# Turned squares of the attention probabilities: sixteen transfers from SBUF to SBUF in the place of five through DRAM

## The chip, the cores and the metric

The kernel runs on one core of one Trainium2 chip. The metric is the device time of one execution in microseconds; the median of three runs stands for it. The engines are called as the profile calls them: PE (matrix multiply; PEld is its weight load), DVE (vector), ACT (scalar), POOL (GpSimd) and SP (sync, which here only issues transfers). A `q` behind a name (SPq, ACTq) marks the engine's own queue of instructions, where transfers are issued and semaphores are waited for.

## The reference

```python
xn = _layernorm(x)                                   # x: 4 x 512 x 512
q = einsum('bpd,hde->bphe', xn, W_Q) + b_Q           # 16 heads of 128; k and v alike
scores = einsum('bqhe,bkhe->bhqk', q, k) / sqrt(128)
attn = softmax(where(causal, scores, -100000.0))
z = einsum('bkhe,bhqk->bqhe', v, attn)
s = einsum('bqhe,hed->bqd', z, W_O) + b_O
g = silu(down(silu(gate(xn) * gate_s) * (up(xn) * up_s)) * down_s)   # 512 -> 1408 -> 512
return x + s * g
```

All of it is float32.

## The kernel before

Every float32 factor of a product is kept as a high and a low part (`Split`, line 28), and a product is three matrix products: high x low, high x high, low x high (`mm3`, line 90). The attention runs first, over 8 groups of 2 heads and, in each group, over the 4 batch rows: 64 rounds, which this text calls heads, of about 14.8 us. The feed-forward part follows from about 973 us on and isn't touched.

The order of the instructions on each engine is the order in which the program writes them (`tc.manual_schedule()`, line 461). One round of the loop at line 525 does, for head n:

- `softmax` (line 272): the scores on PE, the row minimum of the negated scores on DVE (line 298), the exponentials on ACT (line 312), the division by the row sum on POOL (line 316). The causal half is left out, so 10 blocks of 128 x 128 (`NS`) stand in the tile `p`.
- `turn_p` (line 319; line 556 calls it): z needs the probabilities with keys on the partitions. DVE transposes squares of 32 x 32 into the tile `sq` (line 330, six instructions). A square is then turned in itself but still lies on the 32 partitions (`b`) of its queries; it must move to the partitions (`a`) of its keys. That move is what the change is about.
- `split_p` (line 346): reads the moved squares, the tile `ptr`, and makes the high part (ACT, line 357) and the low part (DVE, line 358) in two halves, each of two of the four `b`. From the fifth head on it runs right behind the *next* head's `turn_p`, and in the first heads ahead of it, before or after the softmax.
- the loads of the partial sums of the output (`a`, line 401), of weights (line 130) and of weights to look at (line 438), all issued by ACT; the projections of q and k of the next head on PE, brought out by ACT (line 252) and DVE (line 255); then `attend` (line 376) of the head before, twelve matrix products with `pth` and `ptl`; in every second head `project_out` (line 404) of the four tiles of a batch row, whose sums SP stores (line 414), two in the first half of the round and two in the second.

What bounds the buffers: `sq` has one buffer, so DVE's next transposes (line 330) wait until the moves have read it. `ptr` has two. SP issues its transfers in program order: per head the move of the squares and, in every head after the first few, two stores of line 414.

Semaphores are placed by the framework. In the compiled program every transfer that SP or ACT issues raises one of eight completion counters. They are handed out in rotation over both queues together, in the order in which the compiler lays the instructions out, and a transfer is not issued before the one that last had its counter has landed. An instruction that needs more than its own wait is preceded by instructions that only wait, for up to two counters each.

Of the kernel before, what the change touches and what calls it, by code (L numbers as in the profile page):

```python
# [10 lines left out]
F32 = mybir.dt.float32  # L11
# [31 lines left out]
def kernel(  # L43
# [21 lines left out]
    nc = tc.nc  # L65
# [10 lines left out]
    dram = ctx.enter_context(tc.tile_pool(name="dram", bufs=1, space=bass.MemoryType.DRAM))  # L76
# [19 lines left out]
    with ExitStack() as at:  # L96
# [169 lines left out]
        Q = 32  # L266
        NQ = P // Q
        NS = NT * (NT + 1) // 2
# [50 lines left out]
        def turn_p(of):  # L319

            sq = pp.tile([P, NQ, NS, Q], F32, name="sq", tag="sq")
            for pack in PACK:
                for t in pack:
                    for j in range(0, t + 1, 2):
                        n = min(2, t + 1 - j)
                        s0 = slot[j] + t - j
                        step = slot[j + 1] + t - j - 1 - s0 if n > 1 else 1
                        src = of[t][:, j * P : (j + n) * P]
                        dst = sq[:, :, s0 : s0 + (n - 1) * step + 1 : step, :]
                        nc.vector.transpose(  # L330
                            dst.rearrange("p a s i -> p s a i"),
                            src.rearrange("p (s a i) -> p s a i", s=n, i=Q),
                        )
            by_query = dram.tile([NQ, Q, NQ, NS * Q], F32, name="turn", tag="turn", bufs=2)
            nc.sync.dma_start(
                out=by_query.rearrange("b j a s -> (b j) (a s)"),
                in_=sq.rearrange("p a s i -> p (a s i)"),
            )
            raw = pp.tile([P, NQ, NS * Q], F32, name="ptr", tag="ptr", bufs=2)
            for a in range(NQ):  # L340
                nc.sync.dma_start(
                    out=raw[ts(a, Q)], in_=by_query[:, :, a, :].rearrange("b j s -> j b s")
                )
            return raw

        def split_p(raw):
# [114 lines left out]
        with tc.manual_schedule():  # L461
# [57 lines left out]
            inexact, before, raw = None, None, None  # L519
# [5 lines left out]
            for n, (g, b, i) in enumerate(heads):  # L525
# [27 lines left out]
                half = NT // 2 if nxt is not None else NT - 1  # L553
                fill(range(0, half))
                if nxt is not None:
                    raw_next = turn_p(of)
# [38 lines left out]
                if nxt is not None:  # L595
                    *_, kT = project(nxt[1], nh, wk[nh], bk_sb, "k")
                    raw = raw_next
# [206 lines left out]
```

## Time and profile before

| what | us |
|---|---|
| median of the three runs | 1223.08 (1222.31 to 1223.1) |
| the profiled execution's own time | 1222.41 |
| its span in the profile | 1220.6 |
| issues of line 335, 640 KB each | 63, median 3.8 to landing |
| issues of line 341, 160 KB each | 252, median 3.4 to landing |
| DMA traffic over the span | 215.55 MB, mean 177 GB/s |

The span runs from the first to the last instruction of the profiled execution; a time is compared with a time, a span with a span. A busy figure is the time in which an engine had an instruction at work. Counts behind an x are instructions. A line of the stretches view gives, after the stretch and its length, the busy times of PE, PEld, DVE, ACT and POOL with their counts, PE's granted clock, the share of time in which the 16 DMA engines were busy, and the GB/s that they moved. A line of a timeline gives start, duration, engine, line and operation; instructions of one kind in a row are merged, and "x4" is then four of them. A line of the wait list says who waited for whom: the total, how often, the longest.

### The profile page before, as it was taken

The numbers are of one execution on the slowest core, as the hardware profiler recorded it, in microseconds if no ns is written. First come the engines' busy times: TensorE is split into PE (matmuls) and PEld (weight loads), VectorE is DVE, ScalarE is ACT, GpSimd is POOL, SyncE is SP. The second block draws the span as 40 slices with busy tenths as digits, with TensorE's granted clock in tenths as the row PEclk, the third lists the DMA queues.
The fourth block names the chain that finished last, engine by engine and source line by source line (L and its number), as shares of the span: only waits on it lengthen the run. The fifth ranks groups of instructions, "written<-read, shape, count | busy, mean of one in ns | idle before, by whom it ended". The sixth has DMA issues, their size and how long they took to land.

```text
span 1220.6 us, 18887 instructions
## 1 busy us (share of the span) xinstructions
PE 1206.5 (99%) x6514; PEld 1052.7 (86%) x6514; DVE 827.1 (68%) x2044; ACT 525.3 (43%) x1169; POOL 301.7 (25%) x433
## 2 busy tenths in 40 slices
PE   8999999999999999999999999999999999999997
PEld 8888888888888888888888888888888888888886
DVE  6897777777777777777877676767677533434343
ACT  5654444444445445444544454445444342323231
POOL 4212321232123213321412141214121341212010
PEclk9999999999999999999999999999999999999999
DMA  4454456656665667566655565555544893627241
GB/s 161 138 175 147 145 165 206 206 179 190 190 207 174 203 198 218 181 208 192 211 182 173 178 189 175 177 185 173 173 156 156 272 317 93 207 87 213 80 147 38
DMA packets 117912, 215.55 MB, mean 177 GB/s; under 512 B 13232, under 2 KB 45744, under 8 KB 117808
## 3 DMA queue, kind: packets, MB, share of 16 engines
q1 hardware_dynamic: 74016, 134.51, 34.4%
q10 hardware_dynamic: 29376, 53.26, 14.2%
q0 software_dynamic: 14416, 26.48, 7.9%
q8 instruction: 53, 0.87, 0.3%
q14 instruction: 51, 0.42, 0.1%
HBM read 135.17 MB, written 79.04 MB: 175 GB/s over the span
## 4 chain that ended last, share of the span: by engine, by line
PE 95%; DVE 3%; ACT 1%; DMA 0%; issue 0%; SPq 0%; DVEq 0%; ACTq 0%
PE z L387 10%; PE pd L667 7%; PE pg L667 7%; PE pu L667 7%; PE pso L91 5%; PE psv L91 5%; PE pso L92 5%; PE pso L93 5%; PE psv L93 5%; PE psv L92 5%; PE psq L91 5%; PE psq L92 5%; PE psq L93 5%; PE psk L91 5%; PE psk L92 5%; PE psk L93 5%
## 5 line engine op out<-in xcount | busy, mean ns | idle before, releaser
L316 POOL TENSOR_SCALAR p<-p,rtot 128x512 f32<-128x512 f32 (+3 forms) x256 | 148.2, 598 | 675.1 <-DVE rtot L315 675.1
L312 ACT ACTIVATE p<-p,nmax 128x512 f32<-128x512 f32 (+3 forms) x256 | 140.9, 552 | 147.3 <-DVE nmax L298 147.3
L358 DVE TENSOR_TENSOR ptl<-ptr,pth 128x640 fp32r<-128x640 f32 x126 | 133.7, 1099 | 1.4 <-ACT pth L357 1.4
L330 DVE STREAM_TRANSPOSE sq<-p 128x256 f32<-128x256 f32 x378 | 113.3, 361 | 0.0
L298 DVE CUSTOM_DVE_ANT_0 p<-sc,mask 128x512 f32<-128x512 f32 (+2 forms) x192 | 96.5, 552 | 0.3 <-PE sc L93 0.3
L252 ACT ACTIVATE k<-psk,consts 128x512 fp32r<-128x512 f32 (+1 forms) x65 | 44.2, 681 | 108.7 <-PE psk L93 108.6
L252 ACT ACTIVATE q<-psq,consts 128x512 fp32r<-128x512 f32 (+1 forms) x65 | 44.3, 682 | 97.2 <-PE psq L93 72.6
L357 ACT CAST pth<-ptr 128x640 fp32r<-128x640 f32 x126 | 84.9, 724 | 0.1
L413 DVE TENSOR_TENSOR a<-pso,a 128x512 f32<-128x512 f32 x108 | 72.1, 686 | 17.7 <-PE pso L93 16.4
L255 DVE SCALAR_TENSOR_TENSOR k<-psk,consts,k 128x512 fp32r<-128x512 f32 (+1 forms) x65 | 48.0, 739 | 52.8 <-ACT k L252 52.7
L693 DVE SCALAR_TENSOR_TENSOR hd<-pu,consts,sg 128x512 f32<-128x512 f32 x44 | 33.0, 751 | 66.8 <-PE pu L667 62.2
L315 DVE RECIPROCAL rtot<-tot 128x1 f32<-128x1 f32 x256 | 41.6, 162 | 42.7 <-ACT p L312 36.3
L91 PE MATMUL sc<-k,q 128*128 128x512 f32 (+2 forms) x192 | 65.7, 342 | 1.7 <-DVE xl L225 1.7
L93 PE MATMUL sc<-k,q 128*128 128x512 f32 (+2 forms) x192 | 64.7, 337 | 0.0
L92 PE MATMUL sc<-k,q 128*128 128x512 f32 (+2 forms) x192 | 64.7, 337 | 0.0
L255 DVE SCALAR_TENSOR_TENSOR q<-psq,consts,q 128x512 fp32r<-128x512 f32 (+1 forms) x65 | 47.6, 732 | 7.6 <-ACT q L252 7.6
L312 ACT ACTIVATION_READ_ACCUMULATOR p<-p,nmax 128x1 f32 x256 | 47.8, 187 | 0.0
L91 PEld LDWEIGHTS sc<-k,q 128*128 128x128 f32 x192 | 36.2, 188 | 7.9 <-DVE xl L225 3.5
L723 ACT ACTIVATE o<-o 128x512 f32<-128x512 f32 (+1 forms) x17 | 10.3, 607 | 68.8 <-DVE o L722 68.8
L92 PEld LDWEIGHTS sc<-k,q 128*128 128x128 f32 x192 | 36.2, 189 | 3.6
L93 PEld LDWEIGHTS sc<-k,q 128*128 128x128 f32 x192 | 36.1, 188 | 2.6
L691 ACT ACTIVATE sg<-pg,consts 128x512 f32<-128x512 f32 x44 | 30.3, 688 | 17.0 <-PE pg L667 17.0
(734 smaller groups left out, 3811.6 us busy)
## 6 DMA issues: line engine op xcount, KB each, us to landing
turn<-sq SPq DMA_DIRECT2D x63, 640.0 KB, 3.8
ptr<-turn SPq DMA_DIRECT2D x252, 160.0 KB, 3.4
acc<-a SPq DMA_DIRECT2D x124, 256.0 KB, 3.7
a<-acc ACTq DMA_DIRECT2D x108, 256.0 KB, 2.8
xt<-in_x SPq DMA_DIRECT2D x16, 256.0 KB, 4.1
wor<-in_w_o ACTq DMA_DIRECT2D x16, 256.0 KB, 4.5
fa<-acc SPq DMA_DIRECT2D x16, 256.0 KB, 5.9
fx<-in_x SPq DMA_DIRECT2D x16, 256.0 KB, 6.9
```

Source lines behind the costliest of these rows:

```text
L91: nc.tensor.matmul(ps, a.hi, b.lo, start=first, stop=False)
L92: nc.tensor.matmul(ps, a.hi, b.hi, start=False, stop=False)
L93: nc.tensor.matmul(ps, a.lo, b.hi, start=False, stop=last)
L252: nc.scalar.activation(q.hi[:, at_], ps[:, at_], AF.Identity, bias=bias[:, h : h + 1])
L255: nc.vector.scalar_tensor_tensor(q.lo[:, at_], ps[:, at_], bias[:, h : h + 1], q.hi32[:, at_], ALU.add, ALU.subtract,)
L298: nc.vector.tensor_tensor_reduce(out=of[t], in0=where[t], in1=add, scale=-SCALE, scalar=BIG, op0=ALU.add, op1=ALU.min, accum_out=nmax[t],)
L312: nc.scalar.activation(of[t], of[t], AF.Exp, bias=nmax[t], scale=-1.0, accum_out=tot)
L316: nc.gpsimd.tensor_scalar(of[t], of[t], rtot, 1.0, ALU.mult, ALU.mult)
L330: nc.vector.transpose(dst.rearrange("p a s i -> p s a i"), src.rearrange("p (s a i) -> p s a i", s=n, i=Q),)
L358: nc.vector.tensor_tensor(dst(pt.lo), src, dst(pt.hi32), ALU.subtract)
L387: nc.tensor.matmul(o, v, p_, start=k == 0, stop=k == len(todo) - 1)
L667: nc.tensor.matmul(ps, l, r, start=first and k == 0, stop=last and k == len(pairs) - 1)
```

## The change

The sixteen blocks (four key parts `a` by four query parts `b`) are copied one by one from `sq` to `ptr`, 32 partitions with a row of 320 elements (1280 bytes) each. The DRAM tile `turn` is gone. All sixteen are issued by SP, those of the first two `b` ahead of the others.

```diff
@@ turn_p, line 334
-            by_query = dram.tile([NQ, Q, NQ, NS * Q], F32, name="turn", tag="turn", bufs=2)
-            nc.sync.dma_start(
-                out=by_query.rearrange("b j a s -> (b j) (a s)"),
-                in_=sq.rearrange("p a s i -> p (a s i)"),
-            )
             raw = pp.tile([P, NQ, NS * Q], F32, name="ptr", tag="ptr", bufs=2)
-            for a in range(NQ):
-                nc.sync.dma_start(
-                    out=raw[ts(a, Q)], in_=by_query[:, :, a, :].rearrange("b j s -> j b s")
-                )
+            for half in range(2):
+                for a in range(NQ):
+                    for b in (2 * half, 2 * half + 1):
+                        nc.sync.dma_start(
+                            out=raw[ts(a, Q), b, :],
+                            in_=sq[ts(b, Q), a].rearrange("p s i -> p (s i)"),
+                        )
             return raw
```

## The prediction

> **What bounds the kernel now.** I read the page's head and its table by slices first, then busy time by stretches, then PE's own waits.
>
> ```profile
> span 1220.6 us, 18887 instructions
> PE 1206.5 (99%) x6514; PEld 1052.7 (86%) x6514; DVE 827.1 (68%) x2044; ACT 525.3 (43%) x1169; POOL 301.7 (25%) x433
> ...
> 35.00:45.00 10.00, 9.27 (x46) 7.43 (x45) 9.18 (x27) 5.17 (x14) 2.05 (x4) 1.00 0.44 157
> ...
> 60.00:100.00 40.00, 38.33 (x221) 32.98 (x220) 35.57 (x100) 22.02 (x49) 5.64 (x9) 1.00 0.50 156
> 100.00:240.00 140.00, 140.00 (x780) 123.44 (x779) 105.79 (x270) 63.51 (x151) 38.50 (x50) 1.00 0.56 178
> 240.00:600.00 360.00, 360.00 (x2029) 318.75 (x2028) 274.83 (x702) 165.53 (x389) 97.09 (x120) 1.00 0.64 197
> 600.00:960.00 360.00, 360.00 (x2019) 317.95 (x2018) 259.73 (x694) 165.84 (x392) 87.40 (x122) 1.00 0.55 175
> ```
>
> From 100 to 960 us PE is busy for all of the 860 us, at a granted clock of 1.00. While the turned squares are in use (27 to 960 us) PE idles only 0.73 us between 35 and 45 and 1.67 us between 60 and 100: 2.4 us together. The wait list gives these to DVE (`PE sc L91 <- DVE xl L225: 1.7, 4, 0.6` is the largest), none to a transfer of the squares. So removing work around the squares can win at most 2.4 us; the question is whether the new transfers make PE wait.
>
> One head in the middle, from the timelines of SP, DVE and ACT (start, duration, engine, line, what):
>
> ```profile
> 488.62 0.32 SPq L335 DMA_DIRECT2D turn<-sq  x1
> 492.06 1.74 SPq L341 DMA_DIRECT2D ptr<-turn  x4
> 494.86 1.71 SPq L414 DMA_DIRECT2D acc<-a  x2
> ...
> 500.45 0.73 ACT L357 CAST pth<-ptr 128x640 fp32r<-128x640 f32 x1
> ...
> 500.93 1.80 DVE L330 STREAM_TRANSPOSE sq<-p 128x256 f32<-128x256 f32 x6
> 502.65 1.52 DVE L358 TENSOR_TENSOR ptl<-ptr,pth 128x640 fp32r<-128x640 f32 x2
> ...
> 502.76 0.32 SPq L335 DMA_DIRECT2D turn<-sq  x1
> ```
>
> Call T the moment the squares leave (488.62). The last piece back was issued by T+5.2, the first cast that reads it runs at T+11.8, and the next head's transposes refill sq at T+12.3. I read the same marks off all 62 gaps between one turn and the next: medians T+5.6, T+11.6 and T+13.0, a period of 14.8 us; the earliest cast is T+8.1 (first head), the earliest refill T+10.4 (fourth). From T+5.6 plus a landing time (next view) to T+11.6 lie some 2.6 us of slack.
>
> **The change, part by part.** Landing times and issue costs, from the views of tiles sq and ptr and of line 341, and two rows of SP's wait list:
>
> ```profile
> L335 SPq DMA_DIRECT2D turn<-sq x63: 319/320/338, 27.1 to 947.0; - x63
> DMA to landing us min/median/max: 2.9/3.8/6.4
> ...
> L341 SPq DMA_DIRECT2D ptr<-turn x252: 302/424/1266, 30.1 to 953.5; - x126
> L341 SPq EVENT_SEMAPHORE  x97: 17/28/4845, 30.0 to 947.4; - x97
> DMA to landing us min/median/max: 2.3/3.4/5.9
> ...
> SPq L341 <- DMA turn<-sq: 230.0, 63, 6.1
> SPq L414 <- DMA ptr<-turn: 0.8, 1, 0.8
> ```
>
> *Removed:* per head one 640 KB write, four 160 KB reads, and SP's wait for the write (230.0 / 63 = 3.65 us). Nothing of it lies on PE's path: value zero, bounds 0 and -2.4 us. The DMA engines lose half of the squares' traffic (640 KB per head each way), which relieves the weight loads; those too are waited for by nobody on PE's list.
>
> *Added:* sixteen issues of 40 KB (32 rows of 1280 B). Four ptr issues take 1.74 us, of which the last is 0.42, so starts are 0.44 apart; sixteen need 7.04 us where five and a wait needed 5.6. Bounds for one issue are 0.30 and 1.27; I take 0.44, the row with the same row length on the same queue. Landing: no row shows SBUF to SBUF. Bounds are 2.3 and 6.4 from the two tiles; I take 2.3, the fastest 160 KB piece, because a piece is now a quarter of that and no longer shares 1.74 us with three others. Last landing T+7.04+2.3 = T+9.3, with 2.3 us to the median cast and 3.7 to the median refill. The first cast needs only the first eight: T+5.8.
>
> The wait rows speak of what else can delay: an acc store (L414) waited for ptr, which it neither reads nor writes. That is the rotation of eight completion counters over the transfers of SP and ACT together. With sixteen transfers the ninth and later ones of a head wait for earlier ones. If two of the eight are held by ACT's loads and the acc stores, six are left: 16/6 x L of latency plus 6 x 0.44 = 2.6 us. With L = 2.3 that is T+8.7, less than the 9.3 of issuing, so the counters don't bind.
>
> *Moved on SP:* the two late acc stores (T+6.2 here) now queue behind the sixteenth issue, T+7.0 plus; in the first two heads four x loads do. The `a` buffer of such a store is wanted again two heads later, over 20 us on; x of those loads is read by statistics 8 us later or more. Cost nothing.
>
> *Moved on ACT:* ACT issues its loads of a, weights and look ahead of T (500.39 to 501.68 for T=502.76; 4.7 to 2.8 us ahead in the other kind of head). By the compiled order of before, these now share the rotation with the first few of the sixteen and with the stores just ahead, so the last of a head's ACT loads waits for a store issued up to 1.4 us before T (landing 3.7, so about T+2.3) or for the first to fourth new transfer (T+2.7 to T+4.1). Behind it in ACT's queue stand the evictions of q and k (502.99 and 505.71), the last of which feeds the scores at 510.24: k needs ACT 0.69 and DVE 0.75, so may start as late as T+6.0, q 0.7 before it. Holding ACT to T+2.3 or T+4.1 is covered by that; beyond T+5 PE pays one for one.
>
> *Other waits:* the casts, the subtracts and the refill each wait for up to eight counters, two to an instruction, where one to two instructions were enough: some ten waits of 21 to 28 ns per head on DVE and ACT, 0.25 us, hidden under PE from 100 us on. In the DVE-bound first 100 us (DVE 35.57 of 40 us busy) at most 4 x 0.25 = 1.0 us shows; I take 0.3. In the first head the second cast (35.9 us) would start at 27.08+9.3 = 36.4, 0.5 late, but its subtract starts at 37.9 behind another: covered by 0.8.
>
> The Trainium skill speaks against the change: its page "DMA: Bandwidth & Descriptors", section "Rules for kernel authors", says that transfers below 64 KB pay mostly overhead and should be merged, and the page's fit of 2.0 us plus bytes over 436 GB/s makes 2.1 us of 40 KB. Paid one after another that would be an estimate of 33.5 us a head, 20.5 beyond the refill, 62 times: 1270 us more. The rows above show four transfers issued within 1.74 us and landing after 3.4, so the overhead overlaps and the rule's serial reading does not hold here.
>
> *Sum:* span 1220.6 + 0.3 = 1220.9. The profiled execution took 1222.41, 1.8 more than its span; the median of the runs shown, 1223.08, is 0.67 above that. Forecast: 1223.08 + 0.3 = 1223.4.
>
> **The rivals.**
> *A, the sixteen land too late.* Place: the refill of sq and the casts of the next head. If a small transfer takes L = 4.0 rather than 2.3, the counters bind: 16/6 x 4.0 + 2.6 = T+13.3, against a median refill at T+13.0: 0.3 x 62 = 19 us, 1242. It decides from L = 3.9; turn's median of 3.8 is close, ptr's 3.4 gives T+11.7 and nothing. With L = 5 it would be T+15.9 and 180 us. An issue of 0.67 instead of 0.44 (16 x 0.67 + 2.3 = 13.0) does the same without the counters. Against it: 3.8 belongs to 640 KB.
> *B, ACT is held.* Place: ACT's loads of look and weights, which stand before the evictions. If the store or transfer ahead on the counter lands 1.5 us later than I think, ACT is held to T+5.6, 0.6 past the point; in the twenty or so heads with looks and weights this is 12 us: 1235. For it: stores have landed in 3.7 at the median, not the minimum. Against it: k's eviction waits 2.03 us for PE anyway.
> *C, faster.* Less traffic brings the first 100 us forward by up to all of PE's 2.4 us: 1220.7. Against it: those waits are for DVE.
>
> **How the numbers follow.** Forecast 0.60, A 0.20, B 0.15, C 0.05. About 0.2% (2.4 us) is what a measurement of this kernel can tell from no change; the forecast lies within, A and B above, C at the lower edge. Faster 0.05, same 0.60, slower 0.35. The range goes from 1221.5 to 1245: it holds the forecast, B's 1235 and A's 1242, and leaves out A's upper half (0.10), B's tail (0.03) and C (0.05).
>
> **What would show it.** Right: PE busy 360.00 in both long stretches, sixteen issues on SP some 7 us long, landings near 2.3, casts still at T+11 to T+12.6, and no PE wait on ptl or pth. Wrong: SP idle on new transfers within the sixteen and landings near 4 (A); q and k evictions later than T+5 with PE waiting on k's low part (B); the waits on xl gone (C). A piece issue far from 0.44 us would break the sum first.

## The result and the profile after

The changed kernel takes 1233.71 us (median of six runs, 1230.01 to 1238.04); the kernel before took 1222.97 beside it (six runs, 1221.77 to 1223.79). The ratio is 1.009, with a 95% interval of 1.0069 to 1.011: slower by 10.7 us. The runs of the changed kernel scatter over 8 us, those of the kernel before over 2. The profiled execution is the slowest of the six (1238.04, span 1236.3), so its losses are at the upper end of what a run shows.

The head of its page:

```profile
span 1236.3 us, 19954 instructions
PE 1212.9 (98%) x6514; PEld 1056.2 (85%) x6514; DVE 830.3 (67%) x2044; ACT 528.7 (43%) x1169; POOL 300.0 (24%) x433
```

The stretches of the changed kernel, with the same columns as before the change (length, busy PE, PEld, DVE, ACT, POOL, granted clock, DMA share, GB/s):

```profile
60.00:100.00 40.00, 36.30 (x201) 31.27 (x200) 33.83 (x94) 20.37 (x42) 7.12 (x10) 0.96 0.37 107
100.00:240.00 140.00, 139.95 (x790) 123.55 (x789) 105.64 (x275) 65.03 (x153) 33.39 (x45) 1.00 0.41 123
240.00:600.00 360.00, 355.69 (x1973) 313.05 (x1973) 270.14 (x685) 162.66 (x380) 96.73 (x120) 1.00 0.49 149
600.00:960.00 360.00, 359.99 (x2028) 318.19 (x2028) 263.07 (x694) 166.95 (x394) 90.38 (x124) 1.00 0.43 133
```

PE was busy for all of 240 to 600 us; now it idles 4.31 us there. DMA traffic fell as expected (149 GB/s where it was 197), and nobody profits. Where a head loses is found by setting the start of the first z product of each of the 64 heads against that of the kernel before. Of the 15.7 us between the spans, 1.2 lie at the start, before any square has moved; 6.3 lie in the second and fourth heads (2.45 and 3.89); 7.7 in seven heads between the fifteenth and the thirty-ninth, of which one alone has 3.41 and one 1.90. What is left, 0.5, is spread in steps under 0.15 and behind the last z product.

The new transfers, and who waits for them (view of the tile ptr, durations in ns; then the wait list):

```profile
L338 SPq DMA_DIRECT2D ptr<-sq x1008: 507/589/1739, 28.3 to 972.5; - x168
...
DMA to landing us min/median/max: 1.8/1.9/6.1
```

```profile
ACT pth L355 <- DMA ptr<-sq: 24.8, 23, 3.0
DVE sq L330 <- DMA ptr<-sq: 13.6, 14, 2.4
PE z L385 <- DVE ptl L356: 4.2, 4, 1.7
PE sc L91 <- DVE k L255: 3.7, 2, 2.1
SPq L338 <- DMA acc<-a: 18.8, 18, 2.5
```

An issue takes 0.589 us where I had taken 0.44, and with the time between two of them starts are 0.63 apart: the sixteen span 10.0 us from the first start to the last end at best, 10.6 at the median of the 63 sets and 13.5 at the longest. A piece lands 1.9 us after its issue, faster than the 2.3 that I had taken. DVE and ACT now wait for the pieces, and PE waits four times for the low part that DVE makes of them. Its two waits for k, 3.7 us together, stand ahead of the z products of the second and the fourth head; before, the scores never waited for k.

The head that loses most after the fourth, from the timelines of SP, ACT, POOL, DVE and PE (start, duration, engine, line, what; in brackets the idle time before it and what ended it):

```profile
289.51 13.48 SPq L338 DMA_DIRECT2D ptr<-sq  x16
...
304.31 0.73 ACT L355 CAST pth<-ptr 128x640 fp32r<-128x640 f32 x1 [2.17 <-DMA ptr<-sq]
...
305.64 3.11 POOL L135 TENSOR_TENSOR wo2l<-wor,wo2h 128x512 fp32r<-128x512 f32 x2 [3.79 <-ACT wo2h L134]
...
304.37 1.81 DVE L330 STREAM_TRANSPOSE sq<-p 128x256 f32<-128x256 f32 x6 [2.42 <-DMA ptr<-sq]
306.10 3.33 DVE L356 TENSOR_TENSOR ptl<-ptr,pth 128x640 fp32r<-128x640 f32 x2
...
309.49 0.50 PE L385 MATMUL z<-ptl,v_0h 128*128 128x512 f32 x1 [1.66 <-DVE ptl L356]
```

T is 289.51. The sixteen end at T+13.5, the refill of sq starts at T+14.9 after 2.42 us of waiting, and the two subtracts behind it on DVE take 3.33 us, because POOL splits weights at the same time; PE stands for 1.66 us. In the kernel before the subtracts of this head were just as slow, but started in time; its timelines of DVE and PE:

```profile
295.50 3.56 DVE L358 TENSOR_TENSOR ptl<-ptr,pth 128x640 fp32r<-128x640 f32 x2
...
299.57 0.40 PE L387 MATMUL z<-ptl,v_0h 128*128 128x512 f32 x1
```

They ended at 299.06 and PE read them at 299.57: in this head the cover is 0.5 us, not the two or more of a head in which the pair takes 1.52. In 21 of the 64 heads POOL splits weights beside the subtracts, and all the losses after the fourth head stand in the z product of such a head or are first seen at the start of the next one.

The stall costs PE more than its own 1.66 us. The stretches of five microseconds around it (the granted clock is the third number from the end):

```profile
305.00:310.00 5.00, 3.34 (x18) 2.68 (x17) 5.00 (x8) 2.34 (x5) 3.11 (x2) 1.00 0.77 230
310.00:315.00 5.00, 5.00 (x29) 4.96 (x29) 1.93 (x4) 1.27 (x3) 0.00 (x0) 0.66 0.24 64
315.00:320.00 5.00, 5.00 (x26) 4.30 (x26) 4.12 (x16) 3.70 (x11) 2.24 (x4) 1.00 0.28 68
```

In the next stretch of 5 us the granted clock is 0.66, which is another 5.00 x 0.34 = 1.7 us. 1.66 + 1.7 = 3.4, this head's whole loss.

### The profile page after: what moved, and what is told of

Its sections match the earlier page's. It is cut to its first block, busy times and chain, and to the rows that moved or that the text cites. A ratio compares the mean times of both kernels' runs of the same rounds, so it can differ in the third digit from the quotient of the medians.

```text
span 1236.3 us, 19954 instructions
## 1 busy us (share of the span) xinstructions
PE 1212.9 (98%) x6514; PEld 1056.2 (85%) x6514; DVE 830.3 (67%) x2044; ACT 528.7 (43%) x1169; POOL 300.0 (24%) x433
## 4 chain that ended last, share of the span: by engine, by line
PE 77%; SPq 9%; DMA 6%; DVE 4%; ACT 2%; issue 1%; ACTq 0%; DVEq 0%
SPq L338 8%; PE z L385 8%; PE pd L665 6%; PE pg L665 6%; PE pu L665 6%; PE psv L91 4%; PE pso L91 4%; PE psv L93 4%; PE psv L92 4%; PE pso L93 4%; PE pso L92 4%; PE psq L91 3%; PE psq L92 3%; PE psq L93 3%; PE psk L91 3%; PE psk L92 3%
## 5 line engine op out<-in xcount | busy, mean ns | idle before, releaser
L330 DVE STREAM_TRANSPOSE sq<-p 128x256 f32<-128x256 f32 x378 | 113.7, 365 | 14.8 <-DMA ptr<-sq 13.6
L355 ACT CAST pth<-ptr 128x640 fp32r<-128x640 f32 x126 | 88.9, 725 | 28.3 <-DMA ptr<-sq 24.8
L411 DVE TENSOR_TENSOR a<-pso,a 128x512 f32<-128x512 f32 x108 | 72.1, 687 | 17.7 <-PE pso L93 17.0
L255 DVE SCALAR_TENSOR_TENSOR k<-psk,consts,k 128x512 fp32r<-128x512 f32 (+1 forms) x65 | 48.0, 739 | 42.2 <-ACT k L252 42.0
L91 PE MATMUL sc<-k,q 128*128 128x512 f32 (+2 forms) x192 | 66.6, 347 | 5.5 <-DVE k L255 3.7
L255 DVE SCALAR_TENSOR_TENSOR q<-psq,consts,q 128x512 fp32r<-128x512 f32 (+1 forms) x65 | 47.8, 736 | 12.6 <-ACT q L252 12.6
L91 PEld LDWEIGHTS sc<-k,q 128*128 128x128 f32 x192 | 36.5, 190 | 12.3 <-DVE k L255 4.9
L721 ACT ACTIVATE o<-o 128x512 f32<-128x512 f32 (+1 forms) x17 | 10.3, 607 | 68.8 <-DVE o L720 68.8
```

The source lines that it names most:

```text
L91: nc.tensor.matmul(ps, a.hi, b.lo, start=first, stop=False)
L255: nc.vector.scalar_tensor_tensor(q.lo[:, at_], ps[:, at_], bias[:, h : h + 1], q.hi32[:, at_], ALU.add, ALU.subtract,)
L330: nc.vector.transpose(dst.rearrange("p a s i -> p s a i"), src.rearrange("p (s a i) -> p s a i", s=n, i=Q),)
```

## The experiments

My theory after the first look: what decides is the moment at which the queue that issues the sixteen is done with them, against the refill of sq and the casts. At 0.63 us a piece that moment comes some 3 us later than I had worked out, and the cover is used up. Rivals: the counters and the transfers that share them; the acc stores and the x loads that were moved back on SP; sixteen transfers from SBUF to SBUF costing by their number, whoever issues them. Twelve kernels tell these apart. In the diffs, lines with "-" are those of the changed kernel.

**What makes an issue dear.** The squares go to DRAM as before, and come back in sixteen pieces of the same 32 rows of 1280 bytes.

```diff
+            nc.sync.dma_start(out=by_query..., in_=sq...)
...
-                            in_=sq[ts(b, Q), a].rearrange("p s i -> p (s i)"),
+                            in_=by_query[b, :, a, :],
```

> The write to DRAM as before, but sixteen reads of 40 KB (32 rows of 1280 bytes) in the place of four of 160 KB: the shape of the new pieces with the source of the old ones. If the 0.59 us that one new issue takes comes from SBUF on both sides, an issue here takes about 0.44 us as before and the sixteen take some 7 us; if it comes from the shape of 32 short rows, 0.59 us and 10 us. The last piece lands at T+3.0+7.0+2 = T+12 in the first case and T+15 in the second, against refill at T+13 (which here needs only the write) and casts at T+11.6: some 10 us slower than before in the first case, over 60 us in the second, as the casts then come 3 us late in every head.

The tile's view:

```profile
L343 SPq DMA_DIRECT2D ptr<-turn x1008: 302/419/1922, 30.3 to 971.0; - x168
...
DMA to landing us min/median/max: 1.7/1.9/4.8
```

Same rows, same bytes, same queue: 0.419 us from DRAM, 0.589 from SBUF; of the two issue times the shorter came. So the pair of memories, not the shape of 32 rows, makes the issue 0.17 us dearer, and 0.44 was near the right price, for the wrong kind (starts are 0.46 apart here). The run took 1237.55 us (one run). The casts are late here, in 60 heads by 2.0 us on average (`ACT pth L357 <- DMA ptr<-turn: 122.3, 60, 4.1`), and yet the z products are only 15.1 us behind at the last head, 6.3 of them in the second to fourth heads. So with sq free early a late cast alone is mostly covered from the fifth head on; the first four lose by it as much as in the changed kernel (6.4).

**Which heads lose.** The new move in the first four heads only, and from the fifth on only.

```diff
-        def turn_p(of):
+        def turn_p(of, head):
+            if head < 4:   # the other kernel: head >= 4
...
+            else:          # through DRAM, as before
```

> The sixteen transfers in the first four heads only, the five through DRAM in all others. If the loss of the changed kernel's first four heads (2.45 + 0.12 + 3.89 = 6.5 us by the starts of z) belongs to these heads and is not made later, about 6.5 us remain: 1228 to 1231. If the loss is one of the long middle alone and the early part is chance, 1223 to 1224.

> The five through DRAM in the first four heads, the sixteen transfers in the other 59. The rest of the loss is then left: 7.8 us in the profiled run, in heads 14 to 38, so 1226 to 1231, and e2 and e3 together make up the whole change. If the early heads push the later ones into their loss, 1223 to 1225.

The first: 1228.21 us (1226.91 to 1230.21), ratio 1.0041 (1.0027 to 1.0055), 5.6 us. The second: 1229.19 (1228.33 to 1231.31), ratio 1.0055 (1.0038 to 1.0072), 6.6 us. Together 12.2, where the whole change costs 10.7. Half of the cost belongs to four heads out of 64, those in the DVE-bound first 100 us. The other half lies in few of the sixty heads, seven in the profiled execution of the second kernel, by 0.3 to 2.2 us, and all seven come right behind weight splits.

**More transfers.** The four pieces that go to the last key part are cut in two: twenty a head.

```diff
-                        nc.sync.dma_start(...)
+                        src = sq[ts(b, Q), a].rearrange("p s i -> p (s i)")
+                        cuts = (0, 160, 320) if a == NQ - 1 else (0, 320)
+                        for lo, hi in zip(cuts, cuts[1:]):
+                            nc.sync.dma_start(out=raw[ts(a, Q), b, lo:hi], in_=src[:, lo:hi])
```

> Twenty transfers: the four pieces of the last a are moved in two halves of 640 bytes a row. If the issue rate decides, SP's chain is 20 x 0.63 = 12.6 us at the least, the last piece lands at T+13.9, the refill takes 1.8 more, and no head can be shorter than 15.7 us, where 14.8 is the mean before: 0.9 x 60 = 54 us and the first heads' loss on top, some 1280 to 1300, more where a transfer waits for its counter. If the loss is one of single unlucky heads, four more transfers add a few us: 1235 to 1240.

1348.93 us (1348.53 to 1349.96), ratio 1.1041 (1.1022 to 1.1059). Four more issues cost 115 us more than the sixteen did, 1.8 per head, more than the size that I had expected. Its wait list:

```profile
DVE sq L330 <- DMA ptr<-sq: 153.1, 50, 5.1
...
PE z L385 <- DVE ptl L356: 59.0, 40, 2.8
```

The refill waits in 50 heads, and PE stands 59.0 us for the low part; the rest of the loss is the lower clock behind the stalls (0.973 over the span) and other waits. Sixteen stood at the edge; twenty are past it in nearly every head.

**Fewer issues on SP, without touching another queue.** The first two `b` move from SBUF to SBUF in eight pieces, the other two through DRAM in one write and four reads.

```diff
-            for half in range(2):
+            half = NQ // 2
...
+            nc.sync.dma_start(out=by_query..., in_=sq[half * Q :]...)
             for a in range(NQ):
-                    for b in (2 * half, 2 * half + 1):
+                for b in range(half):
                     nc.sync.dma_start(out=raw[ts(a, Q), b, :], in_=sq[ts(b, Q), a]...)
+            for a in range(NQ):
+                nc.sync.dma_start(out=raw[ts(a, Q), half:, :], in_=by_query[:, :, a, :]...)
```

> The pieces of the first two b go from SBUF to SBUF in eight transfers, the others through DRAM in one write ahead of them and four reads behind them: 13 issues on SP, 0.3 + 8 x 0.63 + 4 x 0.44 = 7.1 us, sq free at T+7.3, the last piece at T+9.2. If the issue rate of the sixteen is the cause, nothing is late from the fifth head on and the time is 1223 to 1226. If any use of transfers between SBUF and SBUF on this queue hurts, half of the loss stays: about 1228.

1222.08 us (1221.41 to 1223.52), ratio 1.0003 (0.9993 to 1.0012): the time of before. The stretches:

```profile
240.00:600.00 360.00, 360.00 (x2029) 318.72 (x2028) 275.21 (x702) 166.09 (x389) 97.08 (x120) 1.00 0.56 174
600.00:960.00 360.00, 360.00 (x2019) 317.92 (x2018) 260.51 (x694) 166.44 (x392) 87.37 (x122) 1.00 0.50 153
```

**The rotation of the counters.** ACT's loads and the acc stores are issued by POOL, so that the sixteen share their counters with hardly anything.

```diff
-                nc.scalar.dma_start(out=a, in_=acc_d[b][t])
+                nc.gpsimd.dma_start(out=a, in_=acc_d[b][t])
-            nc.sync.dma_start(out=acc_d[b][t], in_=a)
+            nc.gpsimd.dma_start(out=acc_d[b][t], in_=a)
```

(and the weight and look loads alike)

> The sixteen transfers in all heads, but the loads of a, of weights and of looks and the acc stores are issued by POOL, so that in the attention the rotation of the eight counters on SP holds almost nothing but the sixteen. If it is the shared counters that delay the last pieces of heads 14 to 38 by 0.5 to 3.5 us, the sixteen take 10.0 us in every head, land at T+12 and the loss of the middle goes: about 1229 to 1230, of which 6.5 are the first heads. If the cost of sixteen issues is enough by itself, the loss stays at 1233 to 1235.

1259.24 us (1257.07 to 1262.13), ratio 1.0304 (1.0283 to 1.0325): neither case. The sixteen still span 10.0 to 12.8 us, since SP now waits for its own earlier pieces (`SPq L338 <- DMA ptr<-sq: 26.8, 36, 2.2`). The transfers given to POOL made new waits: PE waits 13.7 us for the low part, and 9.3 once at the start of the feed-forward part, whose first loads POOL issued late. A narrower try moves the stores alone:

```diff
-            nc.sync.dma_start(out=acc_d[b][t], in_=a)
+            nc.gpsimd.dma_start(out=acc_d[b][t], in_=a)
```

> Only the stores of the partial sums go from SP to POOL; ACT's loads stay. If the 256 KB stores between the sets of sixteen (their issues and the completion counters that they hold) push the sixteen past the refill in single middle heads, SP needs 10.1 us for the sixteen in nearly all heads, the losses after the fourth head (8 to 10 us) fall to 3 or less, and the time is 1228 to 1231. If the sixteen issues alone or ACT's loads cause them, the losses stay and the time is 1232 to 1236. Both keep the 6 us of the first four heads.

1261.49 us (1258.41 to 1264.17), ratio 1.0319 (1.0301 to 1.0337): again neither case. The spans of the sixteen hardly changed (46 heads under 11 us where there were 38, the longest 12.7 where it was 13.5). Two timeline rows of POOL and one of DVE show what came instead:

```profile
504.29 1.13 POOL L412 DMA_DIRECT2D acc<-a  x2
505.44 2.54 POOL L135 TENSOR_TENSOR wv4l<-wvr,wv4h 128x512 fp32r<-128x512 f32 x2
...
505.94 5.93 DVE L356 TENSOR_TENSOR ptl<-ptr,pth 128x640 fp32r<-128x640 f32 x2
```

The stores put POOL's four weight splits 1.13 us later, right beside the subtracts, which now take 5.93 us for the pair; the head loses 3.98. Five such heads (pairs of 5.6 to 5.9 us) lose 16 us together. These two kernels say that the counters' other users don't set the chain's length; what they say of the losses is clouded by POOL.

**The x loads.** They leave SP for POOL; and, in a second kernel, the splits of the second to fourth heads also come behind their transposes, as they do from the fifth on.

```diff
-            nc.sync.dma_start(out=xt, in_=x[b, ts(t, P), :])
+            (nc.sync if b == 0 else nc.gpsimd).dma_start(out=xt, in_=x[b, ts(t, P), :])
# second kernel also:
-                early = n < HG * HG or nxt is None
-                if n == 1:
-                    pt = split_p(raw)
+                early = n == 0 or nxt is None
```

> Only the x loads of the second to fourth batch row go from SP to POOL, so that they no longer stand behind the sixteen issues. If the late x loads make the early losses (6.3 us over heads 1 and 3 of the changed kernel), these fall to about 3 and the time to 1229 to 1231. If the early losses come from the late casts and refills of the squares themselves, they stay at 6 and the time at 1232 to 1236.

> The sixteen transfers in all heads, but the x of the later batch rows is loaded by POOL, ahead of nothing of SP, and heads 1 to 3 split their squares behind their own transposes, as the later heads do. If the loss of the first heads comes from casts and statistics that stand too near behind the squares' last piece, 5 to 7 us of the loss go: 1226 to 1230, the loss of heads 14 to 38 remaining. If it comes from something else in the first heads, 1232 to 1236.

The first: 1236.0 us (1233.58 to 1238.11), ratio 1.0115 (1.01 to 1.0131). The second: 1233.37 (1229.97 to 1236.6), ratio 1.0088 (1.0061 to 1.0114), a miss. In neither do the statistics wait for x any more between 25 and 100 us, where the changed kernel has `DVE st L187 <- DMA xt<-in_x: 1.3, 2, 0.8`. With x alone the second to fourth heads still lose 5.1 us in the profiled execution, beside 6.4; with the splits moved too, 2.8. So the late x loads are not what the early heads lose by; the place of the splits is a part of it. The second kernel's total didn't follow, because its later heads lost some 10 us, where the changed kernel's profile has 7.7.

**Eight pieces on another queue.** The second half is issued by POOL, so SP's chain is 5 us long.

```diff
-                        nc.sync.dma_start(
+                        (nc.sync, nc.gpsimd)[half].dma_start(
```

> The eight transfers of the first two b stay on SP, the eight of the others are issued by POOL at the same time. If the loss comes from one queue issuing sixteen at 0.63 us each, SP's chain is 5.0 us, the last piece lands near T+7 to T+9, no refill waits, and the time is that of before to within 2 us: 1222 to 1226. If the transfers between SBUF and SBUF themselves are slow, or the sharing of counters with ACT's loads is what counts, it stays above 1230.

1259.02 us (1257.93 to 1259.97), ratio 1.03 (1.0283 to 1.0317), 37 us: a miss. All of the loss lies in seven heads, every eighth (4.0 to 7.6 us each); the other 57 lose nothing but 0.9 at the start. The timelines of POOL and ACT in one of the seven:

```profile
487.85 3.52 POOL L338 DMA_DIRECT2D ptr<-sq  x7 [2.54 <-DVE sq L330]
494.14 0.50 POOL L338 DMA_DIRECT2D ptr<-sq  x1 [2.78 <-PE psv L93]
494.65 1.27 POOL L135 TENSOR_TENSOR wq8l<-wqr,wq8h 128x512 fp32r<-128x512 f32 x1
495.87 1.27 POOL L135 TENSOR_TENSOR wk8l<-wkr,wk8h 128x512 fp32r<-128x512 f32 x1
...
495.96 0.34 ACTq L130 DMA_DIRECT2D wqr<-in_w_q  x1
...
498.04 0.69 ACT L252 ACTIVATE q<-psq,consts 128x512 fp32r<-128x512 f32 x1 [10.78 <-POOL wk8l L135]
```

POOL's transfers stand ahead of its weight splits, the eighth 2.78 us late; ACT's next load into wqr waits until the split has read it; and q's eviction, behind that load in ACT's queue, starts 10.78 us after ACT's last work. What held the eighth transfer isn't settled: the row names a product that it doesn't read.

**Twelve pieces and four copies.** The four blocks with a equal to b keep their partitions, so POOL copies them, ahead of the splits too.

```diff
-                        nc.sync.dma_start(...)
+                        src = sq[ts(b, Q), a].rearrange("p s i -> p (s i)")
+                        if a == b:
+                            nc.gpsimd.tensor_copy(raw[ts(a, Q), b, :], src)
+                        else:
+                            nc.sync.dma_start(out=raw[ts(a, Q), b, :], in_=src)
```

> The four blocks that keep their partitions (a equal to b) are copied by POOL, and only twelve are transferred, with no DRAM between. If the length of SP's chain is what counts, 12 x 0.63 + 1.9 - 0.1 = T+9.4 for the last landing, as early as with half of the move through DRAM, and the time is that of before, 1221.5 to 1224, PE busy 360.0 in both long stretches. If transfers from SBUF to SBUF cost the time by something other than the length of the chain (counters, ACT's loads held up, SBUF traffic), three quarters of them leave 5 us or more: 1228 and above. A rival of its own: POOL's copies, in order among its other work, come later than the transfers, and the refill waits for them: 1226 or more with DVE waiting on POOL.

1231.93 us (1231.64 to 1232.92), ratio 1.0078 (1.0064 to 1.0092): a miss. Nobody waits for a transfer of ptr in the steady part. The loss again lies in seven heads, the same ones as with eight pieces on POOL, 0.9 to 1.7 us each (the third head loses another 1.0), and PE waits for k there (`PE sc L91 <- DVE k L255: 7.1, 7, 1.5`). The copies, 2.95 us for the four, stand where POOL's transfers stood.

**All sixteen, with POOL's eight behind the splits.** This is the run that separates the length of the chain from all the rest.

```diff
-                        nc.sync.dma_start(
-                            out=raw[ts(a, Q), b, :],
-                            in_=sq[ts(b, Q), a].rearrange("p s i -> p (s i)"),
-                        )
+                        src = sq[ts(b, Q), a].rearrange("p s i -> p (s i)")
+                        if half == 0:
+                            nc.sync.dma_start(out=raw[ts(a, Q), b, :], in_=src)
+                        else:
+                            later.append((raw[ts(a, Q), b, :], src))
...
                 split_pending(n)
+                for dst, src in later:
+                    nc.gpsimd.dma_start(out=dst, in_=src)
+                later.clear()
```

> All sixteen pieces, eight issued by SP and eight by POOL, but POOL's eight after the round's weight splits. If only the length of one queue's chain costs, and the 37 us of the kernel with eight on POOL ahead of the splits came from the splits behind them, every head is covered (SP done at T+5, POOL's last issue at some T+8, landing by T+10) and the time is 1221.5 to 1225. If sixteen transfers cost by their number whoever issues them (counters, landings), losses of the changed kernel's size stay: 1230 or more.

1222.02 us (1221.73 to 1223.34), ratio 0.9997 (0.9988 to 1.0006): the time of before. Its timelines of SP, POOL and DVE in one of the heads that lost most with the other order:

```profile
489.78 4.96 SPq L342 DMA_DIRECT2D ptr<-sq  x8
...
490.06 1.88 POOL L135 TENSOR_TENSOR wq9l<-wqr,wq9h 128x512 fp32r<-128x512 f32 x1
491.90 1.87 POOL L135 TENSOR_TENSOR wk9l<-wkr,wk9h 128x512 fp32r<-128x512 f32 x1
493.71 3.98 POOL L562 DMA_DIRECT2D ptr<-sq  x8
...
489.63 2.99 DVE L359 TENSOR_TENSOR ptl<-ptr,pth 128x640 fp32r<-128x640 f32 x2
```

The subtracts are as slow as ever beside the splits (2.99), the pieces are the same sixteen, and they land later than in the changed kernel (2.3 us at the median, where it was 1.9). But SP is done at T+5, POOL at T+7.9. Sixteen transfers cost nothing by their number; one queue issuing them for 10 us and more does.

This kernel settles a rival that the two on the rotation left clouded. POOL's pieces take their counters from a set of eight of POOL's own, so it could be the easier rotation that helped, and not the shorter chain. But SP waited more for the stores here than in the changed kernel (18.8 us in 18 places there):

```profile
SPq L342 <- DMA acc<-a: 31.7, 26, 2.8
```

Single sets of SP's eight take up to 8.4 us where 4.9 is the least. So the waits for counters are still there, and behind a chain of 5 us they cost nothing.

Open: a second buffer for sq, which should take the refill's wait away, wasn't tried. That a loss needs both the late chain and the slow subtracts is read from the traces; no kernel moved the splits away from the subtracts. Why the losing heads differ from run to run isn't known.

## Why the prediction was right or wrong

The forecast of 1223.4 us, held at 0.60, missed by 10.3. The 1233.71 lies inside the range only because the range was drawn wide enough for the rivals, and that it stands near B's 1235 is luck: B's mechanism did not come.

*PE as the bound, nothing to gain: right.* No kernel is faster than before by more than its interval. PE is busy for all of 100 to 960 us before, so a move that is done in time is worth nothing; the relief of the DMA engines shows (149 for 197 GB/s) and buys no time.

*"sixteen need 7.04 us": wrong, and this is the step that failed.* I took 0.44 us for an issue, the row with the same row length on the same queue, which was a read from DRAM. Measured: 0.589, starts 0.63 apart, 15 x 0.63 + 0.59 = 10.0 us where no piece waits. The first kernel shows why that row didn't carry over: the same pieces read from DRAM cost 0.419. My own bounds (0.30 to 1.27) held it; the choice between them was by shape, and the kind of memory decided. The prediction did name this: a piece issue far from 0.44 would break the sum first.

*Landing 2.3: close, on the safe side.* It was 1.9. Without a wait the last of the sixteen starts at T+9.45 and lands at T+11.4, not at T+9.3; the median of the 63 sets lands at T+12.1. Heads whose refill of sq doesn't wait start it mostly at T+12.1 to T+13.5, so some 1 to 2 us of cover are left, where I had counted 3.7 to the median. The Trainium skill's fit, cited in the prediction, gave 2.1 for the landing; its page has it for transfers issued by GpSimd, and these were issued by SP. The rows have 1.9, and the serial reading remains refuted, since sixteen pieces were done within some 11.4 us.

*"so the counters don't bind": wrong in single heads.* SP waits 18.8 us in 18 places for acc stores within the sixteen (2.5 at most), which together with single slow issues (up to 1.74) stretches the ten microseconds to 13.5 in the worst heads. This is a part of the cause in the middle: in six of the seven heads that lose there the sixteen take 11.8 to 13.5 us and land at T+13.1 to T+14.8, past a refill due at some T+12.4, which the T+11.4 of issuing alone would have met. In the first head no piece waits, and the length of the issues is enough by itself. Freeing the rotation of other users hardly shortened the chain, as SP then waited for its own pieces. With the 7.04 us that I believed in, even the longest stretch of 3.5 gives a landing at 7.04 + 3.5 + 1.9 = T+12.4, just in time, which is an estimate.

*Moved on SP: "cost nothing" was right for the time.* The x loads did come later and were waited for, by 1.3 us in all, which contradicts the 8 us that I counted on; but taking them away left the early loss. Outside SP's own queue no instruction waited for an acc store.

*Moved on ACT: right.* ACT was held ahead of q's eviction, 17.7 us in six heads, 3.8 at the longest, and PE didn't wait for q or k after the first 100 us. The cover was thin, though, as the kernels with work put ahead of POOL's splits showed.

*The first heads, "+0.3 us": wrong by 5 to 6.* The cover of 0.8 us for the second cast was worked out with T+9.3. With T+11.4 that cast waited 2.95 us, and k, behind it on DVE, held the scores for 1.64:

```profile
39.88 0.73 ACT L355 CAST pth<-ptr 128x640 fp32r<-128x640 f32 x1 [2.95 <-DMA ptr<-sq]
...
47.71 0.50 PE L91 MATMUL sc<-k,q 128*128 128x512 f32 x1 [1.64 <-DVE k L255]
```

*Rival A came, by its side condition.* The text named it: an issue of 0.67 does the same without the counters. Its place (refill and casts) is what the wait list shows, its price is not: 19 us was an even 0.3 for 62 heads. In truth most heads stay covered, and the cost falls on the DVE-bound first heads and on those where POOL's splits slow the subtracts, by up to 3.9 us a head. I had worked with medians of the slack over 62 heads, and it is the thinnest heads that pay. B and C did not come.

## What to carry to other kernels

Price a transfer's issue from a row with the same pair of memories, not the same shape, and add all issues of the queue up to the moment that its single buffer is wanted again. Compare that moment with the slack of the thinnest head, not the median one: here a pair of subtracts that took 3.3 us instead of 1.52 decided where the time was lost. If a long chain must be shared, look at what stands behind the new work on the second queue: eight pieces on POOL ahead of its weight splits cost 37 us, and behind them nothing.

## What the runs showed of the hardware

- A stall of PE of 1.66 us was followed by a granted clock of 0.66 in the next stretch of 5 us, so it cost twice its length. Stalls of 1.64 us (to 47.7 us) and 1.63 us (to 491.8) in the same execution had no such effect, nor had one of 1.94 us in the kernel with the new move from the fifth head on. So the length of a stall alone doesn't decide, and what does isn't shown. The Trainium skill, page "TensorE: Matmul & The Clock Gate", section "Why this matters for your kernels", asks for no gaps of more than about 3 us; here one of about half that was already followed by a drop.
- DVE's subtract of two SBUF tiles and POOL's split of weights hold each other up: the pair of subtracts took 1.52 us alone, 2.6 to 3.6 beside two or three splits in the kernel before and up to 5.93 beside four in a row, while a split went from 1.27 to 1.88. The Trainium skill, page "SBUF — State Buffer", section "SBUF: two separate sides", states such a lock between a DVE instruction with two SBUF inputs and a POOL instruction that reads SBUF; these rows agree.
- An issue on SP took 0.589 us from SBUF to SBUF and 0.419 from DRAM to SBUF, for the same rows and bytes; the landing was 1.9 us for both.
